# A four-layer graph network on one core: fewer doubled columns in the weight generation, and another order for the additions beside it

## The chip, the cores and the metric

The kernel runs on one core of one Trainium2 chip. The metric is the device time of one execution in microseconds; lower is better. It is measured in several runs, and their median is given. A separate execution is recorded by the hardware profiler; all views below are of that one execution.

## What is computed

The input is x (8 batches, 2048 nodes, 64 features) and a sparse, row-normalised adjacency matrix of 2048 x 2048. Four layers follow one another, each of the form x = x + layer(relu(layernorm(x)), adj). The change lies at the seam of the first two. Layer 0 is a graph convolution whose weights differ from node to node: they are generated from a 16-wide embedding of the node.

```python
def _L0_gnn_ref(x, A, embedding, weight, bias):
    K = weight.shape[1]                                   # 3
    w = jnp.einsum('nd,dkio->nkio', embedding, weight)    # weights of each node
    b = jnp.einsum('nd,do->no', embedding, bias)          # bias of each node
    As = [jnp.eye(N, dtype=x.dtype)]
    if K > 1:
        As.append(A)
    for _ in range(2, K):
        As.append(2.0 * (A @ As[-1]) - As[-2])
    A_stack = jnp.stack(As, 0)
    x_g = jnp.einsum('knm,bmc->bnkc', A_stack, x)         # the terms
    out = jnp.einsum('bnki,nkio->bno', x_g, w)
    return out + b
...
h = jnp.maximum(_layernorm(x, axis=-1), 0.0)
x = x + _L0_gnn_ref(h, adj, L0_gnn_embedding, L0_gnn_weight, L0_gnn_bias)
h = jnp.maximum(_layernorm(x, axis=-1), 0.0)
x = x + _L1_gnn_ref(h, adj, ...)
```

Below, "terms" are the entries of x_g, "y" is the sum out without the bias, and "the block's work" is x + y + b, its layernorm and its relu, which the second layer starts from.

## The kernel before

**The stages.** From the start to about 281 us the adjacency products of layer 0 are made and the terms are written to DRAM (TD). From there to about 526 us the node groups run: this is the stage that the change touches. From about 526 us on the adjacency matrix is loaded again and layers 1 to 3 run on it.

**The node groups.** The 2048 nodes are 16 groups (g) of 128. The loop at lines 1333 to 1347 goes over the groups, and inside over six slots (i from 0 to 5). In slot i it calls `make_w(g + 1, i)`, which generates a sixth of the weights of the next group, then `apply_w(g, i)`, which multiplies the terms of this group by its weights, then `beside(g, i)`, which does a piece of the block's work. A block is four groups, 512 nodes. The weights of group 0 are generated ahead of the loop (lines 1180 to 1190), between the last matmuls of the terms.

**Generation (`make_w`, lines 1152 to 1174).** Sixteen TensorE matmuls (eight steps o of two row halves r, 64 rows each, float32r) take a 64x128 piece of `wg` as the stationary operand and the group's embedding `E` as the moving one. Each matmul is needed for 128 columns of the result. With `wide` at 2 (line 1161) the same embedding is sent twice, so that 256 columns are written; the second 128 are overwritten by the next step. This is so in six of the eight steps; the two others stand at the end of a PSUM bank. Then VectorE (half 0) and ScalarE (half 1) copy the two PSUM tiles `gen` to the weight buffer `w`. There are three `gen` tiles of two banks each, and each slot takes two.

**Application (`apply_w`, lines 1238 to 1266).** Slots 0 and 3 run 64 small matmuls on the third term (shown as yb<-w,t), the other slots 32 on the first two terms (yb<-w,tt). After slots 2 and 5 ScalarE and then VectorE copy `yb` to `ys`. After slot 5 GpSimd issues four DMAs that store `ys` to `yD` in DRAM, one for each quarter.

**Loads.** At the start of iteration g, `load_group(g + 1)` (lines 1137 to 1142) issues on SyncE's queue the loads of the next group's terms: `tt`, and two for `t`. Each has two buffers, so they wait until group g - 1 has been applied. `load_e(g + 2)` issues one load on GpSimd's queue.

**The block's work.** At the end of iteration g with g % 4 == 3, `x1_load(0, g // 4)` (lines 955 to 967) issues on SyncE's queue a load of x (`acc`), one of the bias (`bn`), and four of y (`yt`), which must wait for the four groups' stores to `yD`. The work itself, `x1_pieces` (lines 1268 to 1309), is cut into eleven pieces, and `beside_at` (lines 1311 to 1313) says at which (g % 4, i) the next piece is issued, during the following four groups:

| piece | at (g % 4, slot) |
|---|---|
| acc = acc + yt (VectorE) | (1, 0) |
| acc = acc + bn (VectorE) | (1, 1) |
| mean (VectorE) | (1, 3) |
| z = acc - mean in two instructions (VectorE), its square (ScalarE); acc + b2r and the store of acc to xs (GpSimd) | (1, 4) |
| variance (two of VectorE), rstd as a power (GpSimd) | (2, 0) |
| z times rstd, with relu (VectorE) | (2, 1) |
| two copies to planes of 16 bits (ScalarE), then their store to hp (GpSimd) | (2, 3), (2, 4) |
| transposing loads (SyncE) | (3, 0) |
| two copies of the transposed planes (ScalarE) | (3, 3), (3, 4) |

The last block has no following groups; its work is done after the loop.

**Order.** In this stage every engine's instructions keep the order in which the program issues them (`nc.on`, line 1047)[...]. All of these calls go through a helper that records them, so the profile shows line 67 for nearly every instruction; they are told apart by the names of their tiles.

Of the kernel before, what the change touches and what calls it, by code (L numbers as in the profile page):

```python
# [15 lines left out]
ALU = mybir.AluOpType  # L16
# [59 lines left out]
def uniform_path(  # L76
# [30 lines left out]
    nc = InOrder(tc)  # L107
    P = 128
    B, N, C = x.shape
    NP = B // 2  # L110
    NCH = N // P
    NB = N // 512
# [46 lines left out]
    def block(tag, name, bufs):  # L159

        return work.tile([P, 4, 2 * C], F32, tag=tag, name=name, bufs=bufs)
# [17 lines left out]
    def part(nb):  # L179
        return slice(4 * nb, 4 * nb + 4)  # L180
# [10 lines left out]
    def nodes(acc):  # L191

        return acc.rearrange("p j f -> p (j f)").rearrange("p (e j c) -> p j e c", e=2, c=C)

    def load_x(layer, p, nb, queue=nc.sync):
        acc = block("acc", f"acc_{layer}_{p}_{nb}", 2)
        fill_x(acc, layer, p, nb, queue)
        return acc

    def fill_x(acc, layer, p, nb, queue=nc.sync):  # L200
        if layer == 0:
            return queue.dma_start(runs(acc), runs_of(x, p, nb))
        return queue.dma_start(acc, xs[p][:, part(nb), :])
# [6 lines left out]
    def bits(t):  # L210
        return t.bitcast(U16)
# [16 lines left out]
    def load_planes(layer, p, nb, pool):  # L228
        t = pool.tile([P, 512], F32, tag="hb", name=f"pt_{layer}_{p}_{nb}", bufs=hbufs[-1])
        pt = bits(t).rearrange("f (s n) -> f s n", s=2)  # L230
        for s in range(2):
            nc.sync.dma_start(
                pt[:, s],
                hp[layer][p][nb, s].rearrange("p (t f) -> (p t) f", t=4),
                transpose=True,
            )
        return pt
# [29 lines left out]
    def norm_stages(xt, name, done, out_, fine=False):  # L267

        z = block("z", f"z_{name}", 3)
        g = groups(z)  # L270
        mean = small.tile([P, 8], F32, name="mean")
        nc.vector.tensor_reduce(each(mean), nodes(xt), axis=AX.X, op=ALU.add)
        if fine:
            yield
        for e in range(2):
            firsts.append(nc.vector.scalar_tensor_tensor(
                split(z)[:, :, e], each(mean)[:, :, e, None].to_broadcast([P, 4, C]), -1.0 / C,
                nodes(xt)[:, :, e], op0=ALU.mult, op1=ALU.add
            ))
        sq = block("sq", f"sq_{name}", 1)  # L280
        squares.append(nc.scalar.activation(sq, z, AF.Square))
        yield
        var = small.tile([P, 8], F32, name="var", bufs=3)
        nc.vector.tensor_reduce(var, groups(sq), axis=AX.X, op=ALU.add)
        variances.append(
            nc.vector.tensor_scalar(var, var, 1.0 / C, EPS, op0=ALU.mult, op1=ALU.add)
        )
        rstd = small.tile([P, 8], F32, name="rstd", bufs=3)
        powers.append(nc.gpsimd.tensor_tensor(rstd, var, mhalf, op=ALU.pow))
        yield  # L290
        h = z if out_ is None else out_
        scales.append(nc.vector.scalar_tensor_tensor(
            groups(h), g, 0.0, rstd[:, :, None].to_broadcast([P, 8, C]), op0=ALU.max, op1=ALU.mult
        ))
        done(h)
        yield
# [473 lines left out]
    def feat(i, name):  # L770

        if i == 0:
            return term(1, name)
        return lastp[0].tile([P, 512], F32, tag="fm", name=name, bufs=4)
# [178 lines left out]
    x1s = []  # L953

    def x1_load(p, nb):

        acc = load_x(0, p, nb)
        bn = work.tile([P, 4, C], F32, tag="bn", name=f"bn_{p}_{nb}", bufs=1)
        nc.sync.dma_start(bn, biasD[:, part(nb), :])
        yt = block("z", f"yt_{p}_{nb}", 3)  # L960
        yv = yt.rearrange("(m u) j f -> u m (j f)", u=4)
        for u in range(4):
            nc.sync.dma_start(
                yv[u].rearrange("m (e r) -> m e r", e=2),
                yD[nb][u, 2 * p:2 * p + 2].rearrange("e m t c -> m e (t c)"),
            )
        x1s.append((p, nb, acc, yt, bn))
# [70 lines left out]
    for m in range(NCH):  # L1038
        i = m if m < 9 else m + 3
# [8 lines left out]
    for n, (kind, p) in enumerate(rounds):  # L1048
        own = kind == "a"
        for nb in range(NB if n + 1 < len(rounds) else 0):  # L1050
            i = 4 * n + nb
# [85 lines left out]
    def load_group(g):  # L1137

        cs = slice(g * P, (g + 1) * P)
        nc.sync.dma_start(tts[g % 2], TD[:, :2, :, cs].rearrange("b k i n -> (k i) b n"))  # L1140
        for hf in range(2):
            nc.sync.dma_start(t2s[g % 2][two[hf]], TD[:, 2, :, cs].rearrange("b i n -> i b n"))
# [3 lines left out]
    def gen_tile(g, i, h):  # L1146
        pool = psg if not pys or len(gens) % 3 < 2 else psums[-1]
        tag = "gen" if pool is psg else "genx"
        gens.append(pool.tile([P, 2, 512], F32, tag=tag, name=f"gen_{g}_{i}_{h}"))
        return gens[-1]  # L1150

    def make_w(g, i):

        e = es_[g]
        ps = [gen_tile(g, i, h) for h in range(2)]
        k2 = i > 3
        n0 = 8 * (i - 4 if k2 else i)
        for o in range(8):
            q, n = divmod(n0 + o, D // 2 if k2 else D)
            at = 2 * D * C * k2 + n * P  # L1160
            wide = 1 + (o % 4 < 3)
            for r in range(2):
                rs = two[r]
                multiply(
                    ps[r].rearrange("p a f -> p (a f)")[:, o * P:(o + wide) * P],
                    wg[rs, q, at:at + P], e[rs, None, :].to_broadcast([2 * D * 2, wide, P]),
                    start=True, stop=True,
                )
        w, per = (w2, D) if k2 else (w1s[g % 2], 2 * D)
        for h in range(2):  # L1170
            src = ps[h].rearrange("p a f -> p (a f)").rearrange("p (o n) -> p n o", o=8)
            moved[h] = (nc.vector.tensor_copy, nc.scalar.copy)[h](
                w[:, :, per * h + n0:per * h + n0 + 8], src
            )
# [5 lines left out]
    for k in range(6):  # L1180
        make_w(0, k)
        nb = 1 + k // 2
        for q in range(3 * (k % 2), 3 * (k % 2) + 3):
            m, i = order_l[NCH - KEEP + q // 2], q % 2
# [83 lines left out]
    def x1_pieces(p, nb, acc, yt, bn):  # L1268

        nc.vector.tensor_tensor(acc, acc, yt, op=ALU.add)  # L1270
        yield
        nc.vector.tensor_tensor(
            nodes(acc), nodes(acc), bn[:, :, None, :].to_broadcast([P, 4, 2, C]), op=ALU.add
        )
        yield
        z = []
        n = norm_stages(acc, f"1_{p}_{nb}", z.append, None, True)
        next(n)
        yield
        next(n)  # L1280
        nc.gpsimd.tensor_tensor(
            nodes(acc), nodes(acc), b2r[:, None, None].to_broadcast([P, 4, 2, C]), op=ALU.add
        )
        kept.append(nc.gpsimd.dma_start(xs[p][:, part(nb), :], acc))
        yield
        next(n)
        yield
        next(n)
        yield
        pl = bits(block("sq", f"pl_1_{p}_{nb}", 1).rearrange("p t f -> p (t f)"))  # L1290
        hv = bits(z[0].rearrange("p t f -> p (t f)")).rearrange("p (q s) -> p s q", s=2)
        pl = pl.rearrange("p (s q) -> p s q", s=2)
        for half_ in range(2):
            nc.scalar.copy(pl[:, half_], hv[:, half_])
            if half_:
                nc.gpsimd.dma_start(hp[1][p][nb].rearrange("s p q -> p s q"), pl)
            yield
        pt = load_planes(1, p, nb, typ)
        yield
        out_ = feat(0, f"gT_1_{p}_{nb}")  # L1300
        ov = bits(out_).rearrange("f (t n s) -> f s t n", t=4, s=2)
        for half_ in range(2):
            nc.scalar.copy(ov[:, half_], pt[:, half_].rearrange("f (n t) -> f t n", t=4))
            if half_:
                joined.append(out_)
                ops.setdefault(0, ([], []))[1].append(out_)
                if nb == 0:
                    nc.scalar.copy(out_[:, 0:1], ivt)
            yield

    beside_at = [(1, i) for i in (0, 1, 3, 4)] + [(2, i) for i in (0, 1, 3, 4)] + [
        (3, i) for i in (0, 3, 4)
    ]
    pieces = []

    def beside(g, i):
# [16 lines left out]
    for g in range(NCH):  # L1333
        if g + 1 < NCH:
            load_group(g + 1)
            if g + 2 < NCH:
                load_e(g + 2)
        for i in range(6):
            if g + 1 < NCH:
                make_w(g + 1, i)  # L1340
            apply_w(g, i)
            beside(g, i)
        if g % 4 == 3:
            x1_load(0, g // 4)
        if g == NCH - 2:
            BTs.clear()
            load_again("A", 3)
# [977 lines left out]
```

## Time and profile before

| | us |
|---|---|
| median of three runs | 1182.24 |
| lowest and highest of them | 1176.29, 1182.43 |
| the profiled execution | 1177.22 |
| its span, first to last instruction | 1175.5 |
| mean granted clock of TensorE | 0.975 |

The page gives each engine's busy time over the span, the span in 40 equal slices, and the chain of work that ended last, followed back from the end. The table by windows gives the same busy times for stretches that one chooses. The costliest groups of the stage, by operation and tile (count, then busy time in us, mean ns of one, and idle time before them), and the stage as a whole (window, length, then the busy times of PE, PEld, DVE, ACT and POOL, the granted clock, the DMA share and GB/s):

```profile
L67 PE MATMUL gen<-E,wg 64*128 64x256 f32 (+1 forms) x1536 | 129.4, 288 | 4.3 <-DVE w L67 2.9
L67 PEld LDWEIGHTS gen<-E,wg 64*128 64x128 f32 x1536 | 108.3, 186 | 28.0 <-issue 8.3
L67 DVE COPY w<-gen 128x1024 f32<-128x1024 f32 x96 | 117.5, 1224 | 86.9 <-PE gen L67 86.8
L67 ACT COPY w<-gen 128x1024 f32<-128x1024 f32 x96 | 98.4, 1025 | 135.3 <-PE gen L67 135.3
```

```profile
297.00:526.10 229.10, 217.67 (x5239) 186.89 (x5241) 139.25 (x143) 115.92 (x133) 52.92 (x81) 0.99 0.49 112
```

[...] PE can be shown as busy while a matmul waits. Where that matters, the starts of the records are compared.

### The profile page before, as it was taken

To read this page: it belongs to the slowest core of one execution; us is meant where nothing else is said; L and a number is where in the kernel's file an instruction comes from. 1 tells how busy PE (TensorE), PEld (TensorE's weight loads), DVE (VectorE), ACT (ScalarE), POOL (GpSimd) and SP (SyncE) were. 2 spreads that over 40 slices of the span, in tenths; PEclk is the share of its full clock that TensorE was granted. 3 is DMA by queue.
4 is the path that set the end of the run, shared out by engine and by line. 5 is a ranking of instruction groups with operands and counts; after the bars stand their busy time and mean duration, and the time that the engine had idled before them with its cause. 6 is when DMAs were issued, how large, how long until landed. Compare 5 with 4: busy or idle time off the path is not lost.

```text
span 1175.5 us, 27836 instructions
## 1 busy us (share of the span) xinstructions
PE 1094.4 (93%) x12030; PEld 873.8 (74%) x12030; DVE 628.5 (53%) x1078; ACT 415.2 (35%) x573; POOL 280.0 (24%) x326
## 2 busy tenths in 40 slices
PE   9999899999998999999389998999799999899996
PEld 8778778887887788887257776777567677688875
DVE  5555334412555656661366567646664654455675
ACT  5724322421444455551133533353235233211110
POOL 5514000100011313223203242223222400231121
PEclk9999999999999999999689998999999999999998
DMA  9926567655544364639877558826784563532432
GB/s 354 394 82 198 168 174 175 168 154 178 113 110 106 97 128 105 127 94 364 259 165 171 148 151 210 190 78 168 196 172 98 164 137 96 148 110 53 135 118 75
DMA packets 160196, 186.09 MB, mean 158 GB/s; under 512 B 63048, under 2 KB 114888, under 8 KB 155840
## 3 DMA queue, kind: packets, MB, share of 16 engines
q1 hardware_dynamic: 137872, 110.17, 39.4%
q0 software_dynamic: 15632, 58.84, 14.6%
q10 hardware_dynamic: 6560, 15.21, 4.0%
q8 instruction: 96, 1.57, 0.6%
q14 instruction: 36, 0.29, 0.1%
HBM read 111.81 MB, written 53.22 MB: 140 GB/s over the span
## 4 chain that ended last, share of the span: by engine, by line
PE 57%; DMA 16%; DVE 10%; ACT 5%; issue 5%; POOL 3%; SPq 3%; ACTq 0%; DVEq 0%; POOLq 0%
PE bv L67 23%; PE yb L67 6%; PE gen L67 6%; SPq L67 3%; PE bv_2a L67 2%; PE bv_3a L67 2%; PE bv_1a L67 2%; DMA st<-in_adj_dram 2%; DMA hp<-pl 2%; PE bv_2b L67 2%; DMA yt<-yD 2%; DVE z L67 2%; PE bv_3b L67 2%; PE bv_0a L67 2%; DVE acc L67 2%
## 5 line engine op out<-in xcount | busy, mean ns | idle before, releaser
L67 POOL TENSOR_TENSOR rstd<-var,mhalf 128x8 f32<-128x8 f32 x64 | 108.0, 1687 | 344.9 <-DVE var L67 343.9
L67 DVE COPY w<-gen 128x1024 f32<-128x1024 f32 x96 | 117.5, 1224 | 86.9 <-PE gen L67 86.8
L67 ACT COPY w<-gen 128x1024 f32<-128x1024 f32 x96 | 98.4, 1025 | 135.3 <-PE gen L67 135.3
L67 PE MATMUL gen<-E,wg 64*128 64x256 f32 (+1 forms) x1536 | 129.4, 288 | 4.3 <-DVE w L67 2.9
L67 PEld LDWEIGHTS gen<-E,wg 64*128 64x128 f32 x1536 | 108.3, 186 | 28.0 <-issue 8.3
L67 ACT ACTIVATE sq<-z 128x512 f32<-128x512 f32 x64 | 40.5, 633 | 227.9 <-DVE z L67 178.7
L67 PE MATMUL bv<-BT_C,H 128*128 128x512 f32 x192 | 77.2, 402 | 0.0
L67 PE MATMUL bv<-BT_B,H 128*128 128x512 f32 x192 | 76.3, 397 | 0.6 <-ACT H L67 0.6
L67 PE MATMUL bv<-BT_B,L 128*128 128x512 f32 x192 | 76.0, 396 | 0.5 <-DVE L L67 0.5
L67 PE MATMUL bv<-BT_C,L 128*128 128x512 f32 x192 | 75.9, 395 | 0.2 <-DVE L L67 0.2
L67 PE MATMUL yb<-w,tt 128*32 128x128 f32 x2048 | 73.6, 283 | 2.2 <-issue 2.2
L67 POOL DMA_DIRECT2D yD<-ys x64 | 37.2, 589 | 159.8 <-DVE ys L67 158.1
L67 DVE SCALAR_TENSOR_TENSOR z<-z,rstd 128x512 f32<-128x512 f32 x64 | 46.1, 720 | 52.3 <-POOL rstd L67 52.3
L67 DVE TENSOR_TENSOR g<-bv,crow 128x512 f32<-128x512 f32 x48 | 33.0, 688 | 65.8 <-PE bv L67 65.2
L67 PE MATMUL bv<-BT,H 128*128 128x512 f32 x144 | 59.7, 415 | 7.4 <-ACT H L67 5.7
L67 PEld LDWEIGHTS yb<-w,tt 128*32 128x32 f32 x2048 | 59.5, 167 | 7.8 <-issue 3.2
L67 PE MATMUL bv<-BT,L 128*128 128x512 f32 x144 | 57.9, 402 | 1.9 <-DVE L L67 1.9
L67 PE MATMUL bv<-BT_A,L 128*128 128x512 f32 x144 | 57.6, 400 | 0.0
L67 PE MATMUL bv<-BT_A,H 128*128 128x512 f32 x144 | 57.3, 398 | 0.0
L67 DVE SCALAR_TENSOR_TENSOR junk<-mt,cols,st 128x512 uint8<-128x512 bf16 x64 | 49.9, 779 | 9.5 <-DMA mt<-MD 9.2
L67 DVE TENSOR_REDUCE var<-sq 128x8 f32<-128x512 f32 x64 | 43.5, 680 | 17.3 <-ACT sq L67 17.2
L67 POOL TENSOR_TENSOR acc<-acc,wl 128x512 f32<-128x512 f32 x16 | 21.8, 1363 | 126.5 <-DVE z L67 125.6
(267 smaller groups left out, 2374.0 us busy)
## 6 DMA issues: line engine op xcount, KB each, us to landing
BT<-in_adj_dram POOLq DMA_DIRECT2D x16, 1024.0 KB, 12.1
crow<-crowD SPq DMA_DIRECT2D x64, 256.0 KB, 3.8
st<-in_adj_dram SPq DMA_DIRECT2D x64, 256.0 KB, 4.4
MD<-md ACTq DMA_DIRECT2D x16, 512.0 KB, 3.5
tt<-TD SPq DMA_DIRECT2D x16, 512.0 KB, 5.2
t<-TD SPq DMA_DIRECT2D x32, 256.0 KB, 5.8
xs<-acc POOLq DMA_DIRECT2D x32, 256.0 KB, 3.6
acc<-xs SPq DMA_DIRECT2D x32, 256.0 KB, 3.6
```

Of the source, the lines that this page charges most:

```text
L67: made = f(*args, **how)
```

## The change

Three things are changed.

1. `wide` is 2 only for the generation of groups with g % 4 == 1 (groups 1, 5, 9 and 13, generated during iterations 0, 4, 8 and 12). All other groups' matmuls send 128 columns.
2. `x1_load` is split. Its loads of x and of the bias are issued at slot 1 of each fourth group (g % 4 == 3), while that group is still being applied. Its four loads of y are issued in slot 0 of the next iteration, which is behind `load_group` of that iteration in SyncE's queue. After the last group they are issued at once.
3. The bias is added at slot 4 of the iteration with g % 4 == 0, before y is there, and no longer as a piece of its own after y. The other pieces move up by one place each: the mean to (1, 1), z, its square and the addition of b2r to (1, 3), variance and power to (1, 4), the scaling to (2, 0), the two plane copies to (2, 1) and (2, 3). The place (2, 4) is dropped, and the pieces from (3, 0) on stay. For the last block the bias is added after y as before.

```diff
     def x1_load(p, nb):
 
+        x1_rest(p, nb, *x1_first(p, nb))
+
+    def x1_first(p, nb):
+
         acc = load_x(0, p, nb)
         bn = work.tile([P, 4, C], F32, tag="bn", name=f"bn_{p}_{nb}", bufs=1)
         nc.sync.dma_start(bn, biasD[:, part(nb), :])
+        return acc, bn
+
+    def x1_rest(p, nb, acc, bn):
+
         yt = block("z", f"yt_{p}_{nb}", 3)
...
-            wide = 1 + (o % 4 < 3)
+            wide = 1 + (g % 4 == 1 and o % 4 < 3)
...
         nc.vector.tensor_tensor(acc, acc, yt, op=ALU.add)
-        yield
-        nc.vector.tensor_tensor(
-            nodes(acc), nodes(acc), bn[:, :, None, :].to_broadcast([P, 4, 2, C]), op=ALU.add
-        )
         yield
...
-    beside_at = [(1, i) for i in (0, 1, 3, 4)] + [(2, i) for i in (0, 1, 3, 4)] + [
+    beside_at = [(1, i) for i in (0, 1, 3, 4)] + [(2, i) for i in (0, 1, 3)] + [
         (3, i) for i in (0, 3, 4)
     ]
+    firsts_ = []
+
+    def beside_first(g, i):
+
+        q = g // 4
+        if (g % 4, i) == (3, 1):
+            firsts_.append(x1_first(0, q))
+        if (g % 4, i) == (0, 0) and g:
+            x1_rest(0, q - 1, *firsts_.pop(0))
+        if (g % 4, i) == (0, 4) and g:
+            acc, bn = x1s[0][2], x1s[0][4]
+            nc.vector.tensor_tensor(
+                nodes(acc), nodes(acc), bn[:, :, None, :].to_broadcast([P, 4, 2, C]), op=ALU.add
+            )
...
             beside(g, i)
-        if g % 4 == 3:
-            x1_load(0, g // 4)
+            beside_first(g, i)
+        if g == NCH - 1:
+            x1_rest(0, NB - 1, *firsts_.pop(0))
```

## The prediction

> **What bounds the kernel now.** I read the page's parts 1, 2 and 4 first.
>
> ```profile
> PE 1094.4 (93%) x12030; PEld 873.8 (74%) x12030; DVE 628.5 (53%) x1078; ACT 415.2 (35%) x573; POOL 280.0 (24%) x326
> ...
> PEclk9999999999999999999689998999999999999998
> ...
> PE 57%; DMA 16%; DVE 10%; ACT 5%; issue 5%; POOL 3%; SPq 3%; ACTq 0%; DVEq 0%; POOLq 0%
> ```
>
> TensorE carries the whole; the granted clock is full nearly everywhere. The change lies in one stage, the node groups, so next comes the table by windows there (columns: window, length, busy time of PE, PEld, DVE, ACT, POOL, clock, DMA share, GB/s).
>
> ```profile
> 341.00:356.00 15.00, 14.83 (x362) 12.91 (x359) 9.00 (x9) 7.32 (x8) 2.89 (x5) 1.00 0.50 121
> ...
> 371.00:386.00 15.00, 11.35 (x289) 9.51 (x289) 8.30 (x10) 5.48 (x6) 2.88 (x5) 1.00 0.55 109
> 386.00:401.00 15.00, 12.61 (x304) 10.94 (x303) 9.39 (x12) 7.41 (x9) 6.50 (x8) 0.94 0.44 111
> ```
>
> A quiet group has PE busy 14.83 of 15 us; those with the blocks' work lose 2 to 4 us, and one loses clock. The timeline (start, length, engine, operation, idle before it and who ended that) shows a quiet slot:
>
> ```profile
> 344.99 1.32 PEld L67 LDWEIGHTS gen<-E,wg 64*128 64x128 f32 x16
> 346.39 1.15 PE L67 MATMUL yb<-w,tt 128*32 128x128 f32 x32
> 346.45 1.22 DVE L67 COPY w<-gen 128x1024 f32<-128x1024 f32 x1 [1.19 <-PE gen L67]
> ...
> 348.86 1.23 DVE L67 COPY w<-gen 128x1024 f32<-128x1024 f32 x1
> ```
>
> DVE copies start every 2.41 us (346.45, 348.86). That is the loop: generate, copy (1.22 us), and generate again into the buffer that the copy freed. PE's full row hides short waits of a second-half matmul for that copy. A half group of three slots takes 7.30 us. I took the starts of yb<-w,t from the timeline for all half groups; those above 7.30 exceed it by: group 1 0.83; group 5 1.39 and 2.83; group 6 2.35 and, after it, 1.32; group 9 1.06; group 10 0.89; group 13 0.29 and 1.12; group 14 0.31. Together 12.4 us. Two causes repeat. First y's loads:
>
> ```profile
> 362.88 2.55 SPq L67 DMA_DIRECT2D yt<-yD  x4
> 365.53 1.38 SPq L67 DMA_DIRECT2D tt<-TD  x1
> 366.95 1.27 SPq L67 DMA_DIRECT2D t<-TD  x2
> 372.26 0.40 PE L67 MATMUL yb<-w,t 64*32 64x128 f32 x2 [1.47 <-DMA t<-TD]
> 373.48 1.22 PE L67 MATMUL yb<-w,t 64*32 64x128 f32 x62 [0.82 <-DMA t<-TD]
> ```
>
> The yt load stands in SP's queue until group 3's y has landed in DRAM, and the terms of group 5, whose buffer was free from about 355, stand behind it; PE then waits for t. Second, rstd:
>
> ```profile
> 390.74 0.67 DVE L67 TENSOR_REDUCE var<-sq 128x8 f32<-128x512 f32 x1
> 392.29 1.74 POOL L67 DMA_DIRECT2D yD<-ys  x3 [1.75 <-issue]
> 394.60 1.68 POOL L67 TENSOR_TENSOR rstd<-var,mhalf 128x8 f32<-128x8 f32 x1
> 396.31 0.69 DVE L67 SCALAR_TENSOR_TENSOR z<-z,rstd 128x512 f32<-128x512 f32 x1 [3.03 <-POOL rstd L67]
> 398.20 1.22 PE L67 MATMUL gen<-E,wg 64*128 64x256 f32 x15 [2.31 <-DVE w L67]
> ```
>
> The power stands on POOL behind the y stores and the E load; DVE waits 3.03 us in order, the next w copy with it, and PE 2.31. The stretch after it runs at half clock:
>
> ```profile
> 395.73:399.14 3.41, 1.10 (x16) 1.00 0.11 26
> 399.14:402.55 3.41, 3.41 (x81) 0.50 0.02 5
> 525.43:528.84 3.41, 1.98 (x66) 1.00 0.22 77
> ```
>
> (PE only.) PE busy 1.10 of 3.41 us was followed by a half clock, 1.98 of 3.41 was not.
>
> [...] narrow pairs of the start (side<-BT, same 64x128 shape) begin 110 to 115 ns apart in the records, wide pairs of gen 117 to 125, and the pair after a narrow one loads 108 ns after its predecessor. [...]
>
> **The change part by part.** *Narrow generation.* 12 of 16 groups (72 of 96 gens) send 128 columns in all 16 matmuls, where 12 of 16 sent 256; no instruction goes. A step falls from about 118 to 112 ns; of the seven steps between first and last matmul six are wide: 36 ns each gen, 2.6 us for 72. In two of six slots DVE's copy of ys holds the next w copy, so perhaps a third of that is hidden. I take 2.0; the ends are 0 (all hidden behind copies) and 72 x 6 x 10 ns = 4.3 us (steps of 108). It could lose only through the clock, which is the first rival.
>
> *y's loads behind the terms.* They are the same four SP DMAs; what moves is that tt and two t loads no longer wait for y's store. Group 5's terms would be issued at about 355 and land 5 to 6 us later (the issues' medians are 5.2 and 5.8), some 10 us early. What goes: group 5's 1.39 and 2.83 less a 1.24 us gap that the chain calls issue (378.85), so 2.98; group 9's 1.06; group 13's 1.41. Sum 5.45 us, the after-effects included. Next in the queue behind yt are group 6's terms, whose buffer comes free only at 369.5: yt's wait to about 363 blocks nothing. yt itself lands at 365 to 368 now; were the 1 MB of terms to delay y's store by 2 us, it would land by 370, and DVE wants it at 371.92. x and bn are issued two thirds of a group earlier, behind loads that do not wait; they land some 5 us on (343 to 348 now) and are read 13 us or more later.
>
> *Bias ahead, one piece fewer.* The bias add (0.68) moves to slot 4 of the group before, after a w copy of 1.22 within 2.41: 0.51 left, hidden by PE's loop; without that cover it would cost 3 x 0.68 = 2.0. Mean, z, var, power and scale each move up. The power is now queued at slot 4, ahead of the y stores and the E load, and its reader comes two slots, 4.9 us, later; add of b2r 1.33, xs issue 0.57 and power 1.68 are 3.6 us of POOL within three slots (7.3), so rstd is some 2 us early. The power may not push the y stores: in the second block it would end near 451.7, they begin at 453.06. ACT's two copies of pl (0.61) fall into slots with over 0.7 idle. What goes: 2.35 and 1.32 (half clock) at groups 6 and 7, 0.89 at group 10. Sum 4.56. Group 14's 0.31 (ACT waits for a y store) I leave.
>
> *The end.* yt of the fourth block still comes after the last group; the reload of BT_A follows the last generation, so the tail only moves forward.
>
> Sum: 2.0 + 5.45 + 4.56 = 12.0 us. The profiled execution took 1177.22 (span 1175.5 and 1.7 around it): 1165.2. The median of the three runs stands 5.0 above it, 1182.24, and gives 1170.2. I predict 1168, between the two, since it is open to which of them a new median belongs.
>
> **The rivals.** *Both stalls go* (0.62): 1168, own range 1160 to 1175.
> *Clock halving in the narrow groups* (0.12; slower). A narrow matmul sends half the columns of a wide one in nearly the same step; [...] windows of eleven narrow groups (11 x 14.6 / 3.41 = 47) may fall to half clock. One such window cost 1.32 us at group 7; from nine on the gain of 12 is gone. Every second one: 24 x 1.32 = 32, so about 1200; a third: 16 x 1.32 = 21, about 1189. For it: a stall of about 1 us, such as the issue gap of 1.24, would now meet a less busy array. Against it: the first window of full clock, 6.60 to 10.02, held 42 narrow side matmuls and three others and no half clock followed; in the groups yb adds 1.06 to 1.19 us of each 2.4.
> *One stall comes back in a new place* (0.14): yt lands too late, or the power delays the y stores; 4.5 to 5.5 of the 12 stay: about 1173.
> *The shift is eaten later* (0.12): after the stage PE waits for DMA from 562 to 583 us in any case. If the reloads of BT, not the last y, set that, little arrives: 1179 to 1182. Against it: these reloads are themselves released by the last generations.
>
> **How the numbers follow.** A measurement of this kernel tells about 0.5%, 5.9 us, from no change: faster is below 1176.3. Nearly all of the first case (0.60) and most of the third (0.10) are faster: 0.70. The rest of these and most of the last make 0.17 the same; the clock case and a bit of the last 0.13 slower. The range 1158 to 1185 leaves out the clock case's bulk and a little at the low end, where the issue gaps (0.83 and 1.24) also go and a step is 108 ns.
>
> **What would show it.** In the profile after: gen at 64x128 with the w copies about 2.37 us apart in narrow groups; no wait of yb for t at groups 5, 9 and 13; no wait of z for rstd, and POOL's rstd ahead of yD; clock 1.00 from 281 to the end of the stage; the stage from 281.3 to 526 about 12 us shorter. I am wrong if half-clock windows fill narrow groups, if DVE's acc<-acc,yt waits for its DMA, if the steps stay at 118 ns, or if the stage shrinks and the end does not move.

## The result, and the profile after

| | us |
|---|---|
| before, median of four runs beside those of after | 1179.26 (1175.22 to 1182.43) |
| after, median of four runs | 1163.09 (1158.4 to 1164.8) |
| ratio after to before, 95% interval | 0.986 (0.981 to 0.991) |
| profiled execution before, after | 1177.22, 1164.80 |
| its span before, after | 1175.5, 1162.7 |
| mean granted clock before, after | 0.975, 0.978 |
| node groups, first gen matmul to the end of the last yb, before | 254.3 (281.3 to 535.6) |
| the same after | 242.1 (278.7 to 520.8) |

The change makes the kernel 1.4% faster. Ratios here and below leave out runs far above the fastest of their kernel, medians and ranges do not; in two experiments below (e1_narrow_only and e3_narrow_all) those runs are part of the effect.

In the profiled executions the node groups are 12.2 us shorter. What comes ahead of them is 2.6 us shorter and what follows 2.0 us longer, in code that the change hardly touches. The page after, the lines of parts 1, 2 and 4 that were read before:

```profile
PE 1085.7 (93%) x12030; PEld 867.4 (75%) x12030; DVE 626.5 (54%) x1078; ACT 415.6 (36%) x573; POOL 280.2 (24%) x326
...
PEclk9999999999999999999599999999999999899999
...
PE 58%; DMA 16%; DVE 9%; ACT 6%; issue 4%; POOL 4%; SPq 2%; ACTq 0%; DVEq 0%; POOLq 0%
```

TensorE still carries most of the chain (58%), with the same 12030 matmuls and 8.7 us less busy time. The row of clock digits is no help here: its one low slice, the twentieth, lies behind the groups in both, and the half-clock window of before at 399 us left its slice of 29 us at 0.94, a 9. The table by windows, with the columns as before:

```profile
341.00:356.00 15.00, 14.69 (x369) 12.69 (x361) 8.98 (x9) 7.68 (x9) 2.98 (x6) 1.00 0.49 124
...
371.00:386.00 15.00, 13.96 (x352) 11.95 (x350) 10.84 (x14) 8.10 (x10) 5.13 (x6) 1.00 0.44 109
386.00:401.00 15.00, 14.65 (x363) 12.81 (x362) 8.54 (x8) 8.19 (x10) 5.01 (x9) 1.00 0.51 120
```

The quiet stretch is as full as before. The two stretches with the block's work had PE at 11.35 and 12.61 of 15 us and now have 13.96 and 14.65. The timeline of after where group 5 begins (start, length, engine, operation, and in brackets idle time and its releaser), first SyncE's queue and then TensorE and VectorE:

```profile
351.16 0.36 SPq L67 DMA_DIRECT2D tt<-TD  x1
351.58 2.18 SPq L67 DMA_DIRECT2D t<-TD  x2
360.31 2.62 SPq L67 DMA_DIRECT2D yt<-yD  x3
```

```profile
367.12 1.25 PE L67 MATMUL yb<-w,t 64*32 64x128 f32 x64
...
368.12 0.68 DVE L67 TENSOR_TENSOR acc<-acc,yt 128x512 f32<-128x512 f32 x1
```

The terms of group 5 go out at 351 us, nine microseconds ahead of y's loads, where before they went out behind them at 365.5. The 64 matmuls on t then run in one piece, where before two of them waited 1.47 us and the rest 0.82. The addition of y finds its data there. The other stall, at group 6:

```profile
379.68 1.66 POOL L67 TENSOR_TENSOR rstd<-var,mhalf 128x8 f32<-128x8 f32 x1 [0.44 <-DVE var L67]
...
382.69 0.64 POOL L67 DMA_DIRECT2D yD<-ys  x1 [1.35 <-DVE ys L67]
383.44 0.68 DVE L67 SCALAR_TENSOR_TENSOR z<-z,rstd 128x512 f32<-128x512 f32 x1
```

The power ends at 381.34, 1.35 us before the first y store could start, and z finds it done: the bracket with 3.03 us is gone.

### The profile page after: what moved, and what is told of

The parts are those of the page before. It is cut to its first block, busy times and chain, and to the rows that moved or that the text cites. A ratio compares the mean times of both kernels' runs of the same rounds, so it can differ in the third digit from the quotient of the medians.

```text
span 1162.7 us, 27841 instructions
## 1 busy us (share of the span) xinstructions
PE 1085.7 (93%) x12030; PEld 867.4 (75%) x12030; DVE 626.5 (54%) x1078; ACT 415.6 (36%) x573; POOL 280.2 (24%) x326
## 3 DMA queue, kind: packets, MB, share of 16 engines
q0 software_dynamic: 15632, 58.84, 14.8%
## 4 chain that ended last, share of the span: by engine, by line
PE 58%; DMA 16%; DVE 9%; ACT 6%; issue 4%; POOL 4%; SPq 2%; ACTq 0%; DVEq 0%; POOLq 0%
PE bv L67 22%; PE yb L67 6%; PE gen L67 6%; PE bv_2a L67 2%; PE bv_3a L67 2%; SPq L67 2%; PE bv_1a L67 2%; DMA st<-in_adj_dram 2%; DMA yt<-yD 2%; PE bv_0a L67 2%; PE bv_2b L67 2%; DVE acc L67 2%; PE bv_3b L67 2%; DVE ys L67 2%; PE bv_1b L67 2%
## 5 line engine op out<-in xcount | busy, mean ns | idle before, releaser
L67 PE MATMUL gen<-E,wg 64*128 64x128 f32 (+1 forms) x1536 | 123.7, 282 | 2.1 <-ACT w L67 1.3
L67 PEld LDWEIGHTS gen<-E,wg 64*128 64x128 f32 x1536 | 104.8, 186 | 24.0 <-issue 9.8
```

The source lines that it names most:

```text
L67: made = f(*args, **how)
```

## The experiments

A half group is three slots. Its length is the time between the starts of two successive runs of yb<-w,t, and it is named by the later of the two: "10.13 at group 5, second half" is the stretch that ends where the second half of group 5 begins. Lengths of the stage are from first gen matmul to last yb. Twelve experiments were run, in three sets, two of them on unchanged kernels; the kernel before ran beside each set: 1180.01 us (11 runs), 1181.45 (47 runs) and 1178.67 (7 runs) in the median.

### Columns alone, order alone

`e1_narrow_only` is the kernel before with one line changed, and `e2_order_only` is the changed kernel with that line put back:

```diff
 e1_narrow_only (from before)
-            wide = 1 + (o % 4 < 3)
+            wide = 1 + (g % 4 == 1 and o % 4 < 3)
 e2_order_only (from after)
-            wide = 1 + (g % 4 == 1 and o % 4 < 3)
+            wide = 1 + (o % 4 < 3)
```

> The kernel before with the narrow generation alone. The stage is measured from the first gen matmul to the end of the last yb matmul: 254.3 us before, 242.1 after. My theory ([...] 112 ns against 118): half groups with narrow generation at about 7.21 us where they were 7.30, the waits for t and for rstd still there, stage about 252. Rival 1 (the columns carry most of the gain): stage 246 or less. Rival 2 (fewer columns let the clock fall where PE still stalls): two or more half-clock stretches inside the stage, stage 255 or more.

> The changed kernel with the doubled columns back in every group; only the two changes of order are left. My theory: no wait of yb for t and none of z for rstd, all half groups at 7.30 but for gaps that the chain calls issue, stage about 244. Rival 1 (the columns carry most): stage 250 or more. Rival 2 (a new wait takes their place): a wait for yt or for a y store of over 0.5 us at groups 5, 9 or 13.

Order alone gave 1165.95 us (1161.93 to 1170.54, ratio 0.989, 0.984 to 0.994) and a stage of 243.7, with half groups of 7.30 (but for 7.83 to 8.13 at the second halves of groups 1, 5 and 14) and no wait for t or rstd. It is nearly the whole gain: 10.6 of the 12.2 us of the stage.

Columns alone made the kernel slower: 1193.12 us (1186.74 to 1211.65, eight runs; ratio 1.010, 1.007 to 1.014, without the two longest, of which the profiled execution is one). The half groups were 7.21 to 7.31 up to group 4, as the first theory had it, but for the 8.12 at group 1 that other kernels have too. Then, behind the first wait for t, the clock fell to half and stayed there. The second rival came true. The timeline of TensorE there:

```profile
368.09 0.40 PE L67 MATMUL yb<-w,t 64*32 64x128 f32 x2 [1.36 <-DMA t<-TD]
369.36 2.01 PE L67 MATMUL yb<-w,t 64*32 64x128 f32 x62 [0.86 <-DMA t<-TD]
371.30 1.97 PE L67 MATMUL gen<-E,wg 64*128 64x128 f32 x16
373.19 1.98 PE L67 MATMUL yb<-w,tt 128*32 128x128 f32 x32
375.10 1.97 PE L67 MATMUL gen<-E,wg 64*128 64x128 f32 x16
```

The two brackets are the waits for t that before has too. What differs is what follows: every full piece takes some 2 us, where narrow groups at full clock take 1.1 to 1.4. A slot is 3.81 us and a half group 11.43. The table by windows of this kernel:

```profile
330.00:360.00 30.00, 29.23 (x740) 25.41 (x742) 18.14 (x18) 15.16 (x17) 5.76 (x10) 1.00 0.31 74
360.00:390.00 30.00, 27.77 (x503) 23.93 (x487) 14.22 (x16) 10.49 (x12) 4.74 (x7) 0.65 0.45 100
390.00:420.00 30.00, 30.00 (x476) 25.78 (x472) 13.07 (x14) 10.86 (x13) 8.26 (x12) 0.50 0.44 101
```

In the third line TensorE is shown as busy for all of the 30 us, at a clock of 0.50, and does 476 matmuls instead of 740. Two such stretches stood in the stage, of 68.3 and 54.6 us, and it took 290.7 us.

### How long a half clock lasts, and what ends it

`e7_narrow_before` is the kernel before without any doubled column; `f1_wide_later` has them in other groups:

```diff
 e7_narrow_before (from before)
-            wide = 1 + (o % 4 < 3)
+            wide = 1
 f1_wide_later (from before)
-            wide = 1 + (o % 4 < 3)
+            wide = 1 + (g % 4 == 3 and o % 4 < 3)
```

> The kernel before with 128 columns in all groups, in the old order with its stalls. If it is the doubled columns of groups 5, 9 and 13 that end a half clock: after the first stall (about 369 us) nothing ends it before the stage does; some 21 half groups of 11.4 instead of 7.2 us, the stage about 335 to 340 and the time about 1260 to 1270. Rival, the clock comes back by itself after some 60 us and the place beside the doubled columns was chance: stretches of half clock of about 70 us as with narrow columns in twelve groups, the stage near 290 to 300 and the time near 1195 to 1215.

> The kernel before, in the old order, with doubled columns only for groups with g % 4 == 3, which are generated in iterations 2, 6, 10 and 14 and not in 0, 4, 8 and 12. If the doubled columns end a half clock: it falls at the first stall of group 5 (about 369 us) and is back in iteration 6, after one to two half groups of 11.4 us, some 15 to 25 us later; the same at groups 9 and 13 if it falls there; the stage 262 to 272 and the time 1185 to 1200, against the 290.7 of the stage with doubled columns for g % 4 == 1. Rival, the end of a half clock does not depend on where the doubled columns stand: stretches of 55 us and more, ending in other iterations than 6, 10 and 14; the stage 285 or more and the time about 1195 to 1215.

Without doubled columns: 1229.02 us (1215.04 to 1233.07), stage 304.3. The clock fell at the same first wait, at 369.1 us, and stayed down for 167.3 us, to 536.4, with half groups of 11.41 to 11.45; then it came back in iteration 12, though nothing there differs from iterations 4 and 8. So the stretch is far longer than with doubled columns, as the first theory has it, but "nothing ends it before the stage does" was wrong; the rival's 70 us were wrong as well, and the time lies between the two. The table by windows shows how even the stretch is:

```profile
390.00:420.00 30.00, 30.00 (x480) 25.66 (x476) 13.25 (x14) 10.97 (x13) 8.49 (x13) 0.50 0.41 98
420.00:450.00 30.00, 30.00 (x448) 25.56 (x446) 11.61 (x11) 11.46 (x14) 2.88 (x5) 0.50 0.37 72
450.00:480.00 30.00, 30.00 (x478) 25.77 (x478) 13.90 (x16) 9.87 (x11) 3.37 (x6) 0.50 0.33 68
480.00:510.00 30.00, 30.00 (x480) 25.72 (x480) 13.26 (x14) 11.07 (x14) 8.96 (x13) 0.50 0.36 90
```

With the doubled columns two iterations later: 1193.01 us (1188.76 to 1196.64) and a stage of 267.2, within what the first theory expected. The clock fell at 372.7 and 444.4 us, behind the waits of groups 5 and 9, and was back at 396.6 and 464.9. Iterations 6 and 10, whose gens are the first with doubled columns, begin their applications at 395.6 and 465.1, and their first gens at 393.7 and 463.3. The table by windows there:

```profile
360.00:390.00 30.00, 27.44 (x523) 23.28 (x520) 15.34 (x17) 10.97 (x12) 2.87 (x5) 0.71 0.44 93
390.00:420.00 30.00, 28.13 (x633) 24.57 (x641) 16.89 (x19) 15.08 (x18) 10.10 (x14) 0.89 0.58 122
```

Iteration 6 went by at half clock where its columns were not doubled, in e1_narrow_only and in e7_narrow_before (0.50 from 390 to 420 us in both tables).

In the records of these runs the clock changes at steps of 3.41 us (the half clock of before from 399.14 to 402.55 us is one), so every such window can be sorted by whether a doubled matmul starts in it. Over the node groups of eight profiles (the kernel before twice, and the six experiments on its order that lost clock there):

| half-clock windows | number | of these the last of their stretch |
|---|---|---|
| without a doubled matmul | 95 | 2 |
| with 6 to 12 doubled matmuls | 11 | 10 |

All three long stretches that met doubled columns (e1_narrow_only's first, and both of f1_wide_later) ended with the first window that held any: 6, 12 and 12 of them. Two ended without: e1_narrow_only's second and that of e7_narrow_before. So in these runs full clock was held without doubled columns (the narrow half groups ahead of the first wait ran at 7.21 us), and once it was lost, it was back behind 10 of the 11 windows that held some, at a cost of some 7 ns a step, and behind 2 of the 95 that held none. What ended those two stretches was not found, and by what the clock goes, these runs do not show.

`e3_narrow_all` asks the same of the changed order, where the waits for t and rstd are gone:

```diff
 e3_narrow_all (from after)
-            wide = 1 + (g % 4 == 1 and o % 4 < 3)
+            wide = 1
```

> The changed kernel with 128 columns in every group, so that the four wide groups go too. My theory: the half groups of iterations 4, 8 and 12 fall from 7.30 to 7.21 as well, stage 0.7 us shorter than 242.1, no half clock. Rival (these groups need the doubled columns to hold the clock): a half-clock stretch in iteration 0, 4, 8 or 12, each worth about 1.3 us.

Three of its four runs took 1161.65 to 1165.21 us, and the profiled one of these had a stage of 240.1 and no half clock in it, with half groups of 7.20 to 7.22 in iterations 4, 8 and 12, as expected. The fourth took 1279.83 at a mean clock of 0.850. Against 0.978 that is 0.128 x 1279.83 / 0.5, by this estimate some 330 us more at half clock, which would be 29 of the stage's 32 half groups at 11.43 us. That this run fell early in the groups and did not come back is inferred from its clock, since it has no profile; what it fell over, with the waits for t and rstd gone, is not known. The doubled columns in each second group of four cost little here (a stage of 242.1 with them against 240.1), and none of the four runs of the changed kernel fell like this, nor any of the four of e4_swap, which doubles the same columns. That is few to call them safe.

### The two edits of the order, one at a time

`e5_y_behind` and `e6_bias_ahead` each make one of them, with doubled columns everywhere; in the first the loads of x and of the bias stay at the end of the group:

```diff
 e5_y_behind (from before; x1_load split as in the change)
...
             beside(g, i)
+            if (g % 4, i) == (0, 0) and g:
+                x1_rest(0, g // 4 - 1, *firsts_.pop(0))
         if g % 4 == 3:
-            x1_load(0, g // 4)
+            firsts_.append(x1_first(0, g // 4))
+        if g == NCH - 1:
+            x1_rest(0, NB - 1, *firsts_.pop(0))
...
 e6_bias_ahead (from before)
-        yield
-        nc.vector.tensor_tensor(
-            nodes(acc), nodes(acc), bn[:, :, None, :].to_broadcast([P, 4, 2, C]), op=ALU.add
-        )
...
-    beside_at = [(1, i) for i in (0, 1, 3, 4)] + [(2, i) for i in (0, 1, 3, 4)] + [
+    beside_at = [(1, i) for i in (0, 1, 3, 4)] + [(2, i) for i in (0, 1, 3)] + [
...
             beside(g, i)
+            if (g % 4, i) == (0, 4) and g:
+                acc, bn = x1s[0][2], x1s[0][4]
+                nc.vector.tensor_tensor(
+                    nodes(acc), nodes(acc), bn[:, :, None, :].to_broadcast([P, 4, 2, C]), op=ALU.add
+                )
```

> The kernel before with only y's four loads issued in slot 0 of the next iteration, behind the terms; columns and bias as before. If the two order edits are independent, as the prediction added them: the stage falls from 254.3 by 5.45 to about 248.8 us, yb waits nowhere for t, and z still waits about 3 us for rstd at group 6, with half a window at half clock behind it; the time about 1174. Rival, the stalls share one cause (a late y load makes the late rstd too, or the reverse): nearly all of the 10 us goes, and the stage is about 244. Second rival, without the earlier bias add the pieces are pushed later: the rstd wait grows and the stage stays above 251.

> The kernel before with only the bias added in slot 4 of the group with g % 4 == 0 and the later pieces moved up; y's loads stand ahead of the next terms as before. If the edits are independent: the stage falls by 4.56 to about 249.7 us, no wait of z for rstd, no half clock, and the waits of yb for t at groups 5, 9 and 13 stay; the time about 1175. Rival, one shared cause: about 244, or no gain at all, about 254.

y's loads behind the terms: 1170.65 us (1165.78 to 1176.68, 12 runs; ratio 0.992, 0.989 to 0.994), stage 248.2 against 248.8 expected. The waits for t are gone and the stall on rstd stands as it did. The timeline at group 6 of this kernel:

```profile
388.15 1.75 POOL L67 DMA_DIRECT2D yD<-ys  x3 [1.75 <-issue]
389.89 0.57 POOL L67 DMA_DIRECT2D E<-embD  x1
...
390.47 1.67 POOL L67 TENSOR_TENSOR rstd<-var,mhalf 128x8 f32<-128x8 f32 x1
...
392.18 0.69 DVE L67 SCALAR_TENSOR_TENSOR z<-z,rstd 128x512 f32<-128x512 f32 x1 [3.02 <-POOL rstd L67]
...
394.06 1.61 PE L67 MATMUL gen<-E,wg 64*128 64x256 f32 x15 [2.33 <-DVE w L67]
```

The bias ahead: 1174.63 us (1169.63 to 1180.9, 20 runs; ratio 0.993, 0.991 to 0.995). The time is as expected; the stage of the profiled execution is not: 254.5 us, as long as before. The stall on rstd is gone in its trace, and what it gave back was lost at the waits for t:

```profile
433.69 0.40 PE L67 MATMUL yb<-w,t 64*32 64x128 f32 x2 [0.93 <-DMA t<-TD]
435.21 2.00 PE L67 MATMUL yb<-w,t 64*32 64x128 f32 x62 [1.11 <-DMA t<-TD]
437.14 1.84 PE L67 MATMUL gen<-E,wg 64*128 64x256 f32 x16
438.91 1.14 PE L67 MATMUL yb<-w,tt 128*32 128x128 f32 x32
```

Here a window at half clock follows the wait at group 9 (2.00 and 1.84 us where 1.26 and 1.15 are usual); the profile of before has none there. To see whether that is the edit or chance, both kernels were profiled again, unchanged, as `f3_before_again` and `f4_bias_again`:

> The kernel before, for a second profile. If the waits of yb for t and of z for rstd come from the order of the queues, they stand at the same groups (5, 9, 13 and 6, 10) within 0.3 us, while the windows at half clock behind them fall elsewhere or are more: the profiled execution was at a clock of 0.975 where the median of 47 runs is 0.972, which is two such windows; the stage 254 to 259 us. Rival, the waits themselves wander: other groups, and a sum that differs by several us.

> The kernel before with only the bias ahead and the pieces moved up, for a second profile; its first had three windows at half clock behind the waits for t, and a stage of 254.5 us, though its median stood 6.8 us under that of before. If these windows come by chance: fewer of them behind the same waits, and the stage 249 to 253 us. Rival, the edit itself makes the waits for t fall to half clock: again three windows at groups 5, 9 and 13, and a stage of 254 to 255.

What the half groups exceed 7.30 us by, two halves of a group together, and the windows at half clock within the stage:

| | group 5 | 9 | 13 | 6, 7, 10, 14 | stage | half clock from |
|---|---|---|---|---|---|---|
| before | 4.22 | 1.05 | 1.41 | 4.9 | 254.3 | 399.1 |
| before again | 4.17 | 1.60 | 1.54 | 3.1 | 254.6 | 374.3 |
| bias ahead | 4.22 | 3.80 | 2.85 | 0.2 | 254.5 | 373.8, 435.3, 496.7 |
| bias ahead again | 5.30 | 3.01 | 2.04 | 0.0 | 254.5 | 371.2 (two windows) |

The waits are at the same groups in both profiles of before, and the half clock moved from group 7 to group 5: its place differed between the two executions, that of the waits did not. (What the table leaves out is mainly group 1, with 0.9 to 2.4 us.) The second profile of the bias edit did not repeat the three windows, but its stage was 254.5 again, so neither expectation held whole. Its 20 runs say that most executions gain some 7 us; two profiles say that the node groups gain nothing. Whether the earlier work beside group 5 makes the waits for t longer, or two executions were unlucky, was not settled. With both edits the question falls away: order alone had neither wait.

### What sets the length of a slot

`e8_three` sends up to three times the columns in all groups; `e4_swap` exchanges the engines that copy gen to w, so that half 0, whose tile the next slot takes again, gets the shorter copy (ScalarE's, 1.03 us against VectorE's 1.22); `f2_swap_wide` is the exchange with doubled columns everywhere.

```diff
 e8_three (from after)
-            wide = 1 + (g % 4 == 1 and o % 4 < 3)
+            wide = 1 + min(2, 3 - o % 4)
 e4_swap (from after), f2_swap_wide (from e2_order_only)
-(nc.vector.tensor_copy, nc.scalar.copy)[h](
+(nc.scalar.copy, nc.vector.tensor_copy)[h](
```

> The changed kernel with up to three times the columns (384 in the first and second of each four steps, 256 in the third) in all groups. [...] half groups about 7.7 to 8.2 us, the stage 256 to 270 and the time about 1180 to 1195. Rival, columns beyond 128 cost only the 6 ns a step that 256 cost: half groups 7.3 to 7.4 and the time about 1167.

> The changed kernel with the two copies of a generation exchanged: ScalarE (1.03 us) copies the first half, VectorE (1.22 us) the second. My theory: the second half of each generation waits for the copy of the previous one's first half, so the slower copy sets the slot; with ScalarE there a slot that is not held by the ys copies falls by up to 0.19 us, a half group from 7.21 to 6.7 to 7.0, the stage by 6 to 15 us, the whole to about 1150 to 1157. Rival (TensorE, shown as 93% busy, is the bound): half groups stay at 7.2 and the time stays within 3 us.

> The changed kernel with the two engines of the w copies exchanged and doubled columns in all groups. If the step of the generation still carries the half groups once the copy is shorter: half groups of about 7.15 against 7.05 us with the narrow groups (6 ns a step, 36 ns a gen), the stage about 2 to 3 us longer than 238.8 and the time about 1159. Rival, after the exchange something else sets the half group (the copies of ys or the loads' sequence): 7.05 as with narrow groups, the stage 239 and the time about 1157.

With 384 columns: 1181.57 us (1177.84 to 1187.11, 20 runs), stage 259.1, half groups 7.80; with two times the columns in the same order the stage was 243.7. The starts of the weight loads of successive steps within a gen, in the median, are 112 ns apart where 128 columns are sent, 119 where 256 are, and 167 to 179 where 384 are. From 128 to 256 columns a step costs 7 ns more, from 256 to 384 some 50 to 60. So up to 256 columns the step hardly follows their number (112 to 119 ns), and at 384 it does (167 to 179); the half groups are within the 7.7 to 8.2 us expected, which was the author's estimate, and the rival is out. What sets the shorter steps was not shown by a run.

The exchange gave 1156.71 us (1154.53 to 1158.82, ratio 0.981, 0.977 to 0.985) and a stage of 238.8; with doubled columns everywhere 1159.23 (1156.21 to 1167.56) and 240.0. Most half groups are 6.98 to 7.12 with narrow groups and alternately 7.14 and 7.08 with doubled ones. The quiet stretch of e4_swap by windows:

```profile
341.00:356.00 15.00, 14.36 (x363) 12.59 (x363) 8.77 (x9) 7.31 (x8) 2.88 (x5) 1.00 0.49 130
```

TensorE is shown less busy than in after (14.36 against 14.69 of 15 us; why was not traced), and the quiet half groups are 0.16 us shorter. The loop through the copy is thus one of the limits, though the exchange gave less than was expected of it: a copy shorter by 0.19 us in each of three slots would have been worth 0.57. The exchange also changes the queue in which each copy stands, which was not separated from its length, and what limits the rest was not pursued. The doubled columns cost 1.2 us of stage under the exchange, half of what the first theory expected of f2_swap_wide and more than its rival. e4_swap is the fastest version found; its four runs (1154.53 to 1158.82 us) lie below the median of the changed kernel, 1163.09, though the two were not run side by side.

## Why the prediction was right, and where it was not

**The sum.** It said 12.0 us for the stage and 1165.2 for a profiled execution that starts from 1177.22; the stage gave 12.2 and the profiled execution took 1164.80. That the second number fits as well is in part luck: outside the stage one execution differed from the other by 2.6 us one way and 2.0 the other. The terms can be checked by the half groups, before against after at the same place, less the 0.09 us that each half of a narrow group gains anyway:

| term | predicted | measured |
|---|---|---|
| t at group 5, without its 1.24 us issue gap | 2.98 | 3.3 |
| t at group 9 | 1.06 | 1.0 |
| t at group 13 | 1.41 | 1.4 |
| rstd at groups 6 and 7, with the half clock | 3.67 | 3.7 |
| rstd at group 10 | 0.89 | 0.9 |
| narrow columns and all else (a remainder) | 2.0 | 12.2 - 10.4 = 1.8 |

The remark that a gap called issue stays was right in kind: at group 5, second half, 0.81 us are left of the 1.24, and the like at group 1. At group 14 the delay grew, from 0.31 to 0.79 us. The cause was not tested, but the traces point to one. The page of after counts a DMA queue by the name of instruction (packets, MB, share of the engines' time), as that of before does with the same 96 packets, and the timeline shows the gap at group 5:

```profile
q8 instruction: 96, 1.57, 0.6%
```

```profile
372.94 0.89 PE L67 MATMUL yb<-w,tt 128*32 128x128 f32 x21 [0.50 <-issue]
```

In the 14 profiles, 32 gaps of TensorE of at least 0.3 us between 290 and 530 us are called issue, and every one of them ends 1.2 to 1.6 us after one of these packets has come in, which itself started 5.8 to 12.4 us after the one before it, where the mean in the node groups is 5.6 in before and 5.4 in after. That TensorE waited there for its own instructions is the author's estimate from these times; no run tested it.

The 2.0 us for the columns came out for another reason than the one given. The steps fell to 112 ns as forecast, and the 22 half groups generated narrow beside the applications gained 0.09 us each, 2.0 in all. But the w copies did not come to stand about 2.37 us apart, as the prediction said they would: in the medians of the whole stage VectorE's were 2.47, 2.41 and 2.42 us apart in the three slots of a half group and are now 2.47, 2.32 and 2.42. One slot in three gained it all, and more than the 36 ns of a gen's six steps. Why it is that slot was not traced. Nor is the loop through the copy, from which the prediction worked, the only limit of a slot, as the exchange of the copies shows (0.16 us of a half group for 0.57 us of copies).

**The median.** The prediction put itself between the profile's basis and the median's, at 1168, and after came out at 1163.09: the medians are 16.2 us apart, the profiled executions 12.4. Over the 47 runs of the second set the time goes with the mean clock (correlation -0.70; clocks of 0.966 to 0.980), 957 us for a whole unit of clock by a straight line. A window of 3.41 us at half clock is 0.5 x 3.41 / 1179 = 0.0014 of the mean, so 1.4 us, which fits the 1.32 us read at group 7. Such windows began behind the stalls that the change removes (at 399.1 us in the first profile of before, at 374.3 in the second), and the profiled execution of before had few of them: a clock of 0.975 against a median of 0.972, worth 2.6 us. But the profiled execution of after had a good clock too (0.978 against a median of 0.977, 1.4 us), so that the clock accounts for about 1 of the 3.8 us between the two gains. The rest may be no more than the spread of four runs (1158.4 to 1164.8), of which the profiled one was the longest.

**Narrow columns "could lose only through the clock".** The way was the right one, and the rival built on it was wrong in form. It let windows of the narrow groups fall by themselves, every second or third, at 1.32 us each, and found it unlikely because 42 narrow matmuls had once run without a fall. In no profile did narrow groups fall by themselves: each of the twelve falls in the node groups came behind a window of 3.41 us in which a stall had left TensorE busy for 1.09 to 2.32 us, with narrow and with doubled columns. (The fourth run of e3_narrow_all, which has no profile, may be an exception.) What the narrow groups did was fail to come back: 93 of 95 half-clock windows without a doubled matmul were followed by another. The price was then not a window but a stretch: (11.43 - 7.21) us for each half group until the clock was back, 13 us to the median and 36 to the stage of the profiled execution when the columns are narrowed alone. So the 2.0 us of the sum are not a term of their own. They were there only beside the other two edits, with no half clock in the stage of after; columns alone took 290.7 us for the stage against 254.3. The prediction added them up as if they were independent.

**The window ahead of a half clock.** The prediction had read two such windows of 3.41 us: 1.10 us of TensorE work, with a half clock behind it, and 1.98 us, with none. The other profiles agree in length (3.41 us) and in the clock of 0.50. All ten windows of the 14 profiles' node groups in which TensorE was busy for 1.09 to 1.81 us were followed by a fall, and of those between 1.84 and 2.32 us only two. No fall came behind a window in which it did nothing.

**The other two rivals.** Neither stall came back in a new place: y's addition waits for no DMA and the power is done before the y stores are due, with 1.35 us to spare. The shift was not eaten later: of the 14.8 us by which the stage ends earlier (2.6 of them gained ahead of it), 12.8 reached the end.

**Additive order edits.** The y edit alone measured 6.1 us of stage against 5.45 predicted; the bias edit alone measured none in two profiles, against 4.56; both together 10.6 against 10.0. The sum held for the pair and, in the profiles, not for the second part by itself. In the medians each part gained more than its term, 10.8 and 6.8 us, and the pair 14.1.

## What to carry to other kernels

A stall's price was its wait and the clock that it took along: 2.35 us at group 6 by the wait for rstd and 1.32 us of half clock behind it, and with narrow columns alone half groups of 11.43 us instead of 7.21 until the clock was back. It was back behind 10 of 11 half-clock windows with doubled matmuls and behind 2 of 95 without, so a few doubled columns in a regular place were a cheap insurance here (a stage of 242.1 us with them against 240.1), and an edit that takes columns out should be tried together with those that remove the stalls. In a queue that the trace shows worked off in order (y's loads held the terms of group 5 until 365.5 us, the wait for rstd held the next w copy for 3.03 us), put what waits for a late producer behind what is ready, and look at each wait for what stands behind it. Take the basis of a forecast from many runs: one profile of a kernel with stalls shows one draw of where the half clocks fell (399.1 us in one of before, 374.3 in the other).

## What had not been expected of the hardware

The same instructions in the same loop ran in either of two ways and kept to it: half groups of 7.21 us at full clock, or, for up to 167.3 us, of 11.41 to 11.45 at half clock, with TensorE recorded as busy for 30.00 of each 30 us from 390 to 510 us in e7_narrow_before. Between 128 and 256 moving columns lay 7 ns of a step (112 against 119), and mostly the difference between a half clock that lasted (93 of 95 windows without a doubled matmul were followed by another) and one that ended within a window (10 of 11 with doubled ones were the last of their stretch).

The stretch of 167.3 us is 49 half-clock windows on end. What the clock goes by is not settled by these runs; the row of TensorE in the profile does not tell it, since in before it is full beside a clock of 1.00 (3.42 of 3.42 us from 6.60 to 10.02) and beside one of 0.50 (3.41 of 3.41 from 399.14 to 402.55).
